# A graph network's two attention convolutions: selection matrices built by ScalarE instead of VectorE, and batch weights read from a PSUM bank

## The chip, the cores and the metric

The kernel runs on one core of a Trainium2 chip. A core has five engines, each with its own instruction queue that is worked off in order: TensorE (PE; its weight loads are listed as PEld), VectorE (DVE), ScalarE (ACT), GpSimd (POOL) and SyncE (SP). SP and POOL mainly issue transfers between the chip's main memory and the on-chip memory SBUF. TensorE writes its results into a second on-chip memory, PSUM, which is made of banks of 512 fp32 columns on 128 partitions; VectorE and ScalarE read and write both memories. Engines tell each other by semaphores that a piece of work is done. The metric is the time on the device in microseconds (us), the median of several runs; one further run was profiled.

## The reference

A graph has 12500 nodes with 128 features each and 200000 edges, sorted by their destination. The reference does a normalisation, two transformer convolutions (4 heads of 32), a second normalisation and a tensor product that is summed over the edges. One convolution is, for all edges at once:

```
q = (x @ Wq + bq); k = (x @ Wk + bk); v = (x @ Wv + bv)      # by node, heads x 32
e = ea @ We                                                   # ea: one number an edge
alpha = sum(q[dst] * (k[src] + e)) / sqrt(32)                 # by edge and head
p = exp(alpha - segment_max(alpha, dst)[dst])
w = p / segment_sum(p, dst)[dst]
out = segment_sum((v[src] + e) * w, dst) + x @ Ws + bs
```

The last stage gathers node rows by `src`, multiplies them with nine edge numbers and sums the products by `dst`.

## The kernel before, in words

Edges are worked on in groups of 4 tiles (U) of 128 edges, 391 groups in all. Three stages follow each other: convolution 0, convolution 1 (`conv(li)`), and the tensor product. Each runs once over all groups. In a convolution a step `s` of the loop works on several groups at once, each in another phase; the order of the instructions on every engine is the order in which the program writes them (a manual schedule, no planner).

What happens to group g in a convolution:

- `fetch_kv` (step g-3): GpSimd gathers the rows of k and v by `src`, with four indirect transfers, one a tile (`gather`, line 602, tile `kv`). For odd g the first of them waits for the last matmul of `query(g-3)`; the source calls that a pause for TensorE's results.
- `turn` (step g-2): ScalarE builds the selection matrix `OT` (destination rows by edges): |row - partition| into `off` (line 850), then relu(1 - off) (line 852).
- `query` (step g-1): TensorE multiplies `OT` with a window of q rows (line 823), which gives q for each edge, in two PSUM banks out of a ring of four (`bank`, tile `pq`).
- `scores` (step g): VectorE multiplies q with k (lines 883, 885) and adds up by head (line 887).
- Batches of 8 groups then get the maximum and the weights in nine steps: transposes by TensorE (`tops_turn`, `ends_turn`, `ends_back`, `weights_back`), scans and comparisons by VectorE (`tops_scan`, `ends_chain`, `weigh`), copies and exponentials by ScalarE (lines 917, 948, 949, 973). `weights_back` (line 978) transposes the weights into PSUM and `weights_keep` (line 984) lets ScalarE copy them into the SBUF tile `wt`.
- `messages` (15 or more steps after the group's scores): VectorE multiplies v with the weights (line 839) and writes the weights themselves and their products with the edge number (line 840).
- `hot`, one step ahead of the messages that need it: VectorE compares the numbers 0 to 127 with each edge's destination row in the group's window (`one_hot`, line 595). This is the selection matrix `O`, edges by destination rows, in a ring of three tiles.
- `sum_up` (lines 860, 862): TensorE multiplies `O` with the messages, which sums them by destination, with one more product that carries a sum over the group's border. `keep_sums` (line 867): ScalarE copies the result out of PSUM one step later, and SP stores it.

Beside the edges the loop works on windows of 128 nodes, about one in four steps: in convolution 0 `nodes_asked` (q of convolution 0) and `nodes_between` (mean, transposition, the skip product `x @ Ws`, q, k and v of convolution 1), in convolution 1 `nodes_mixed` (mean, normalisation with a square root by ScalarE, line 727, and a product). The skip product goes to PSUM (line 693) and VectorE adds it to x (line 698).

PSUM in a convolution: `wb` is one bank. It holds the transposed weights `pp` (columns 0 to 127), the small transposes `sm` of `ends_turn` and `ends_back` (columns 128 to 255) and two places for skip products. `nd` is another bank, with three places for transposes of node windows. Four banks are the ring `pq`, two the sums `pa`.

In the tensor product stage ScalarE builds `O`: for each tile |row - 0..127| into `off` (line 1136) and relu(1 - off) over the group (line 1138). There `products` forms four products a tile, by ScalarE (line 1147) and VectorE (lines 1151 to 1162, with one operand in PSUM), and TensorE sums them (line 1171).

Of the kernel before, what the change touches and what calls it, by code (L numbers as in the profile page):

```python
# [491 lines left out]
SLACK = 3  # L492
KVS = 5
REACH = 10
HEAD = 48
KW = 7
MIX = 352
# [36 lines left out]
def sorted_path(ctx: ExitStack, tc: tile.TileContext, sh_: Shared, x, edge_attr, out):  # L534
# [18 lines left out]
    GE = U * P  # L553
# [22 lines left out]

    SPE = mybir.EngineType.SP
    window = lambda t, w: t[w * P:(w + 1) * P, :]
    iob = sh_.iota
    rel_d, RG = sh_.rel_d, 2  # L580

    for i in range(2):
# [8 lines left out]

    def one_hot(pool, g, hot_bufs):

        O = pool.tile([P, U, P], F32, name="O", bufs=hot_bufs)
        nc.vector.tensor_tensor(O, iob[:, None, :].to_broadcast([P, U, P]),  # L595
                                REL[:, g * U:(g + 1) * U, None].to_broadcast([P, U, P]), op=OP.is_equal)
        return O

    def gather(t, rows, g, behind=None):
# [67 lines left out]
    def nodes_between(pool, bank, turned, skipped, w):  # L667

        A = pool.tile([P, SW], F32, name="A", bufs=4)
        s1 = pool.tile([P, D], F32, name="s1", bufs=4)  # L670
        xt = pool.tile([P, D], F32, name="xt", bufs=7)
        st = {}

        def load():
            nc.sync.dma_start(A, window(sum_d[0], w))
            nc.sync.dma_start(s1, window(s1_d, w))
            load_x(xt, w)

        def mean():
            h = node_mean(pool, 0, A)  # L680
            nc.vector.tensor_add(h, h, s1)
            nc.vector.tensor_add(xt, xt, sh_.BS)
            st["h"] = h

        def turn():
            nc.tensor.transpose(turned, st["h"], ident)

        def keep():
            st["hT"] = pool.tile([P, P], F32, name="hT", bufs=3)
            nc.scalar.copy(st["hT"], turned)  # L690

        def project():
            nc.tensor.matmul(skipped, st["hT"], sh_.WS, start=True, stop=True)
            st["at"] = bank()
            nc.tensor.matmul(st["at"][:, 0:AW], st["hT"], sh_.WA, start=True, stop=True)

        def evict():
            nc.vector.tensor_add(xt, xt, skipped)
            st["qkv"] = pool.tile([P, AW], F32, name="qkv", bufs=3)
            nc.vector.tensor_add(st["qkv"], st["at"][:, 0:AW], sh_.BA)  # L700

        def store():
            nc.sync.dma_start(window(kv_d[1], w), st["qkv"][:, QD:AW])
            nc.sync.dma_start(window(q_d[1], w), st["qkv"][:, 0:QD])
            nc.sync.dma_start(window(xs_d, w), xt)

        return [(0, "load", load), (1, "late", mean), (2, "early", turn), (3, "late", keep), (4, "early", project),
                (5, "late", evict), (6, "load", store)]

# [67 lines left out]
    def conv(li):  # L777
# [1 line left out]

        pool = ctx_l.enter_context(tc.tile_pool(name=f"fc{li}", bufs=1))  # L780
        ps = ctx_l.enter_context(tc.tile_pool(name=f"fcp{li}", bufs=1, space=bass.MemoryType.PSUM))
        wb = ps.tile([P, 512], F32, name="wb")
        pp, sm = wb[:, 0:U * BG * H].rearrange("p (u g h) -> p u g h", u=U, h=H), wb[:, 128:256]
        nd = ps.tile([P, 512], F32, name="nd")
        bank = lambda: ps.tile([P, 512], F32, name="pq", bufs=4)
        pps, outs, msgs, pas, asked = {}, {}, {}, {}, {}
        before = pool.tile([1, H], F32, name="before", bufs=2)
# [54 lines left out]
            return msg  # L842

        def hot(g):
            Os[g] = one_hot(pool, g, 3)

        def turn(g):

            off = pool.tile([P, GE], F32, name="off", bufs=1)
            nc.scalar.activation(off, rows[g // RG][:, g % RG * GE:(g % RG + 1) * GE], AF.Abs, bias=sh_.less)  # L850
            OTs[g] = pool.tile([P, U, P], F32, name="OT", bufs=3)
            nc.scalar.activation(OTs[g].rearrange("p u e -> p (u e)"), off, AF.Relu, bias=sh_.one, scale=-1.0)  # L852
# [121 lines left out]

        def weights_back(j):
            n = sizes[j]
            for u in range(U):
                nc.tensor.transpose(pp[:, u, 0:n, :].rearrange("p g h -> p (g h)"),
                                    bst[j]["aT"][0:n * H, u * P:(u + 1) * P], ident[0:n * H, 0:n * H])

        def weights_keep(j):
            n = sizes[j]
            pps[j] = pool.tile([P, U, BG, H], F32, name="wt", bufs=2)
            nc.scalar.copy(pps[j][:, :, 0:n, :], pp[:, :, 0:n, :])  # L984

        ends_at = {starts[j] + sizes[j] - 1: j for j in range(NB)}
        nodes = (nodes_between, nodes_mixed)[li]
# [24 lines left out]
        with tc.manual_schedule():  # L1012
            for s in range(-AHEAD, last):
                ended = [ends_at.get(s - k) for k in range(9)]
                rs = sums.get(s - 2, [])
                stored += len(rs)
                for k, (g, w) in enumerate(windows):
                    if g > stored or s >= NGR and k:
                        del windows[0:k]
                        break  # L1020
                    n = count % 2 * P
                    count += 1
                    for d, place, f in nodes(pool, bank, nd[:, n:n + P], wb[:, 256 + n:256 + n + P], w):
                        plan.setdefault((s + d, place), []).append(f)
                else:
                    windows = []
                run(s, "store")
                q = s + AHEAD
                if 0 <= q < NGR and rs:
                    bq, br = bases(2 * q, 2 * q + 1)  # L1030
                    assert q - rs[0] == LAG + AHEAD + 2
                    store_sums(rs[0], br)
                else:
                    for r in rs:
                        br, = bases(2 * (r + LAG + AHEAD + 2) + 1)
# [12 lines left out]
                if 0 <= s + 3 < NGR:  # L1048
                    fetch_kv(s + 3)

                if ended[2] is not None:
                    tops_keep(ended[2])
                if ended[6] is not None:
                    ends_keep(ended[6])
                if ended[8] is not None:
                    weights_keep(ended[8])
                if 0 <= s + 2 < NGR:
                    turn(s + 2)
                for m in sums.get(s - 1, []):
                    keep_sums(m)  # L1060

                if ended[1] is not None:
                    tops_turn(ended[1])
                if ended[3] is not None:
                    ends_turn(ended[3])
                if ended[5] is not None:
                    ends_back(ended[5])
                if ended[7] is not None:
                    weights_back(ended[7])
                run(s, "early")  # L1070
                for m in sums.get(s, []):
                    sum_up(m, messages(m))
                while hots and hots[0][1] <= s + 1:
                    hot(hots.pop(0)[0])
                if 0 <= s < NGR:
                    scores(s)
                if ended[2] is not None:
                    tops_scan(ended[2])
                if ended[4] is not None:
                    ends_chain(ended[4])  # L1080
                if ended[6] is not None:
                    weigh(ended[6])
                run(s, "late")
                if 0 <= s + 1 < NGR:
                    query(s + 1)
            assert not windows and not hots
# [9 lines left out]
    with tc.tile_pool(name="tp", bufs=1) as pool, \  # L1096
# [34 lines left out]
            gather(hgs[g], hm_d, g, summed.get(g - REACH - 2) if g % 2 else None)  # L1131

        def hot(g):
            off = pool.tile([P, U, P], F32, name="off")
            for u in range(U):
                nc.scalar.activation(off[:, u, :], iob, AF.Abs, bias=REL[:, g * U + u:g * U + u + 1], scale=-1.0)  # L1136
            Os[g] = pool.tile([P, U, P], F32, name="O", bufs=6)
            nc.scalar.activation(Os[g].rearrange("p u e -> p (u e)"), off.rearrange("p u e -> p (u e)"), AF.Relu,  # L1138
                                 bias=sh_.one, scale=-1.0)

        def products(g):
            j = batch_of[g]
# [531 lines left out]
```

## Time and profile before

| | us |
|---|---|
| median of 3 runs (7340.25 to 7360.03) | 7359.88 |
| profiled execution, its own time | 7424.75 |
| its span | 7422.9 |
| gathers of convolution 0, first start to last end | 137.5 to 2506.0 |
| gathers of convolution 1 | 2594.4 to 4961.4 |
| gathers of the tensor product | 5057.1 to 7356.6 |

| engine | busy us | of it |
|---|---|---|
| TensorE | 5031.8 | sums at L1171 1608.3, at L862 1424.7, queries at L823 1125.1 |
| VectorE | 4923.4 | prod 648.2, AL 549.6, O 532.2, msg 531.8 |
| ScalarE | 3053.5 | OT 564.5, off (L850) 560.5, M 495.7, off (L1136) 495.3 |
| GpSimd | 4867.4 | gathers 3291.2 and 1490.6 |

How to read it: a line of the profile's groups names the program's line, the engine and operation, what is written from what with sizes, and how often; then the busy time of all, the mean duration of one, and the idle time of the engine just before them, with what ended most of it. The span is the stretch between the first and the last instruction. "remote" names a release for which the profile has no sender. Where instructions overlap in an engine's pipeline, their busy time divided by their count is less than the mean of one.

### The profile page before, as it was taken

To read this page: it belongs to the slowest core of one execution; us is meant where nothing else is said; L and a number is where in the kernel's file an instruction comes from. 1 tells how busy PE (TensorE), PEld (TensorE's weight loads), DVE (VectorE), ACT (ScalarE), POOL (GpSimd) and SP (SyncE) were. 2 spreads that over 40 slices of the span, in tenths; PEclk is the share of its full clock that TensorE was granted. 3 is DMA by queue.
4 is the path that set the end of the run, shared out by engine and by line. 5 is a ranking of instruction groups with operands and counts; after the bars stand their busy time and mean duration, and the time that the engine had idled before them with its cause. 6 is when DMAs were issued, how large, how long until landed. Compare 5 with 4: busy or idle time off the path is not lost.

```text
span 7422.9 us, 89199 instructions
## 1 busy us (share of the span) xinstructions
PE 5031.8 (68%) x21249; PEld 3219.3 (43%) x21250; DVE 4923.4 (66%) x13362; ACT 3053.5 (41%) x7785; POOL 4867.4 (66%) x4779
## 2 busy tenths in 40 slices
PE   5566666666777646665666666665777787777777
PEld 4454555555555444444454545452233333333332
DVE  5566666777777746666676777774566666666666
ACT  3333333333333223333444444443555555555554
POOL 6676667676666367767666776654566666666664
PEclk8677777787777867777777777777888888888888
DMA  6455555566666445555555555544455555555554
GB/s 186 135 149 150 148 158 160 162 167 164 168 177 174 129 134 138 143 143 143 146 152 152 153 156 160 157 135 121 125 137 142 144 145 147 149 149 151 152 153 116
DMA packets 868134, 1107.31 MB, mean 149 GB/s; under 512 B 143858, under 2 KB 631568, under 8 KB 867603
## 3 DMA queue, kind: packets, MB, share of 16 engines
q0 software_dynamic: 250240, 692.16, 34.6%
q1 hardware_dynamic: 615832, 408.51, 19.8%
q8 instruction: 176, 2.88, 0.2%
q14 instruction: 355, 2.91, 0.1%
q10 hardware_dynamic: 1531, 0.84, 0.0%
HBM read 935.35 MB, written 165.60 MB: 148 GB/s over the span
## 4 chain that ended last, share of the span: by engine, by line
PE 27%; DVE 22%; another core or an unknown queue 17%; issue 15%; POOL 7%; ACT 6%; DMA 3%; SPq 1%; DVEq 0%; POOLq 0%; ACTq 0%
PE pa L862 8%; PE pa L1171 7%; PE pq L823 6%; POOL kv L602 5%; DVE prod L883 3%; DVE msg L839 2%; ACT M L1147 2%; ACT off L1136 2%; PE pa L860 2%; DVE O L595 2%; POOL hg L602 2%; DVE AL L887 2%; DMA kv<-fkv,srcI 1%; DVE tops L970 1%
## 5 line engine op out<-in xcount | busy, mean ns | idle before, releaser
L602 POOL DMA_INDIRECT kv<-fkv,srcI x3128 | 3291.2, 1052 | 1540.4 <-issue 893.0
L602 POOL DMA_INDIRECT hg<-fhm,srcI x1564 | 1490.6, 953 | 904.6 <-issue 506.0
L1171 PE MATMUL pa<-M,O 128*128 128x512 f32 x3128 | 1608.3, 661 | 295.8 <-ACT M L1147 87.5
L862 PE MATMUL pa<-msg,O 128*128 128x136 f32 x6256 | 1424.7, 363 | 374.1 <-issue 135.2
L883 DVE TENSOR_TENSOR prod<-pq,kv 128x256 f32<-128x256 f32 x1564 | 648.2, 416 | 1333.6 <-remote 737.4
L862 PEld LDWEIGHTS pa<-msg,O 128*128 128x128 f32 x6256 | 1108.1, 244 | 770.0 <-issue 549.3
L823 PE MATMUL pq<-qw,OT 128*128 128x132 f32 x6256 | 1125.1, 332 | 430.0 <-remote 124.3
L823 PEld LDWEIGHTS pq<-qw,OT 128*128 128x128 f32 x6256 | 1034.8, 244 | 471.1 <-remote 207.1
L1171 PEld LDWEIGHTS pa<-M,O 128*128 128x128 f32 x3128 | 624.4, 210 | 1042.5 <-issue 659.0
L852 ACT ACTIVATE OT<-off,fone 128x512 f32<-128x512 f32 x782 | 564.5, 722 | 334.0 <-remote 210.3
L1175 DVE TENSOR_REDUCE acc<-pa 128x128 f32<-128x512 f32 x391 | 265.4, 679 | 603.3 <-remote 448.9
L867 ACT COPY acc<-pa 128x136 f32<-128x136 f32 x782 | 203.6, 261 | 998.1 <-remote 489.4
L850 ACT ACTIVATE off<-rows,fless 128x512 f32<-128x512 bf16 x782 | 560.5, 717 | 106.1 <-DMA rows<-rel_d 67.5
L1147 ACT ACTIVATE M<-hg,s 128x128 f32<-128x128 f32 x1564 | 495.7, 388 | 193.3 <-remote 141.9
L887 DVE TENSOR_REDUCE AL<-prod 128x16 f32<-128x528 f32 x782 | 549.6, 703 | 27.1
L839 DVE TENSOR_TENSOR msg<-kv,wt 128x512 f32<-128x512 f32 x782 | 531.8, 680 | 34.0 <-ACT wt L984 17.3
L595 DVE TENSOR_TENSOR O<-fiota,REL 128x512 f32<-128x512 f32 x782 | 532.2, 681 | 9.4 <-PE pa L862 9.4
L1136 ACT ACTIVATE off<-fiota,REL 128x128 f32<-128x128 f32 x1564 | 495.3, 387 | 0.6 <-ACT M L1147 0.2
L1138 ACT ACTIVATE O<-off,fone 128x512 f32<-128x512 f32 x391 | 282.2, 722 | 273.2 <-remote 226.7
L1158 DVE TENSOR_TENSOR M<-hg,sh 128x384 f32<-128x384 f32 x782 | 392.5, 539 | 0.0
L860 PE MATMUL pa<-msg,fCAR 128*1 128x136 f32 x1196 | 286.7, 329 | 0.0
L1123 ACT COPY d<-sh 128x32 f32<-128x32 f32 (+3 forms) x50 | 9.2, 185 | 647.7 <-remote 448.4
(238 smaller groups left out, 5102.7 us busy)
## 6 DMA issues: line engine op xcount, KB each, us to landing
rows<-rel_d SPq DMA_DIRECT2D x390, 256.0 KB
fsum<-acc SPq DMA_DIRECT2D x782, 68.0 KB
qw<-fq SPq DMA_DIRECT2D x782, 66.0 KB
kv<-fkv,srcI POOLq DMA_INDIRECT x3128
hg<-fhm,srcI POOLq DMA_INDIRECT x1564
fout<-acc SPq DMA_DIRECT2D x391, 64.0 KB
fhm<-qkv SPq DMA_DIRECT2D x98, 176.0 KB
A<-fsum SPq DMA_DIRECT2D x196, 68.0 KB
```

The lines of the kernel that those rows point to most:

```text
L595: nc.vector.tensor_tensor(O, iob[:, None, :].to_broadcast([P, U, P]), REL[:, g * U:(g + 1) * U, None].to_broadcast([P, U, P]), op=OP.is_equal)
L602: i = nc.gpsimd.indirect_dma_start(out=t[:, u, :], out_offset=None, in_=rows[:, :], in_offset=bass.IndirectOffsetOnAxis(ap=srcI[:, g * U + ...
L823: asked[g] = nc.tensor.matmul(pqs[g][u // 2][:, u % 2, 0:QD], OT[:, u, :], qw, start=True, stop=True)
L839: nc.vector.tensor_mul(msg[:, :, :, 0:C], kv4(kv, D), wt[:, :, i, :, None].to_broadcast([P, U, H, C]))
L850: nc.scalar.activation(off, rows[g // RG][:, g % RG * GE:(g % RG + 1) * GE], AF.Abs, bias=sh_.less)
L852: nc.scalar.activation(OTs[g].rearrange("p u e -> p (u e)"), off, AF.Relu, bias=sh_.one, scale=-1.0)
L862: nc.tensor.matmul(pas[g], O[:, u, :], msg[:, u].rearrange("p h c -> p (h c)"), start=(u == 0), stop=(u == U - 1))
L883: nc.vector.tensor_mul(prod[:, c, :, 0:C], half[:, :, 0:D].rearrange("p u (h c) -> p u h c", h=H), kv4(kvs[g], 0)[:, c])
L887: nc.vector.tensor_reduce(ALs[j][:, :, i, :], prod, AX.X, OP.add)
L1136: nc.scalar.activation(off[:, u, :], iob, AF.Abs, bias=REL[:, g * U + u:g * U + u + 1], scale=-1.0)
L1147: nc.scalar.activation(M[:, u, 0, :], hg[:, u, 0:P], AF.Copy, scale=s0[:, i * U + u:i * U + u + 1])
L1171: summed[g] = nc.tensor.matmul(pas[g], O[:, u, :], M[:, u], start=(u == 0), stop=(u == U - 1))
```

## The change

- `one_hot`, called in all three stages now, builds `O` on ScalarE as the tensor product stage did: four |.| instructions into `off` and one relu(1 - off). VectorE's comparison is gone. `off` is one tile that `turn` and `one_hot` share in a convolution. The ring of `O` stays three tiles there (`HOTS`) and six in the last stage.
- `weights_keep` and the tile `wt` are gone. `weights_back` writes the weights of batch j into place j % 2 of `wb`, and `messages` reads them there.
- `wb` now holds two places for weights and one for skip products. While the gathers of the edges run (s below NGR) skip products go there, after that into the ring `pq`. `sm` moves to the fourth place of `nd`.
- Within a step, `messages` is written ahead of TensorE's transposes and of the node work placed "early"; `sum_up` stays behind these.

```diff
 def one_hot(pool, g, hot_bufs):
+    off = pool.tile([P, U, P], F32, name="off")
+    for u in range(U):
+        nc.scalar.activation(off[:, u, :], sh_.iota, AF.Abs, bias=REL[:, g * U + u:g * U + u + 1], scale=-1.0)
     O = pool.tile([P, U, P], F32, name="O", bufs=hot_bufs)
-    nc.vector.tensor_tensor(O, iob[:, None, :].to_broadcast([P, U, P]),
-                            REL[:, g * U:(g + 1) * U, None].to_broadcast([P, U, P]), op=OP.is_equal)
+    nc.scalar.activation(O.rearrange("p u e -> p (u e)"), off.rearrange("p u e -> p (u e)"), AF.Relu,
+                         bias=sh_.one, scale=-1.0)
     return O
...
 # nodes_between
-    nc.tensor.matmul(skipped, st["hT"], sh_.WS, start=True, stop=True)
+    st["skip"] = skipped()[:, 0:D]
+    nc.tensor.matmul(st["skip"], st["hT"], sh_.WS, start=True, stop=True)
...
 # conv
-    wb = ps.tile([P, 512], F32, name="wb")
-    pp, sm = wb[:, 0:U * BG * H].rearrange("p (u g h) -> p u g h", u=U, h=H), wb[:, 128:256]
+    wb = ps.tile([P, 4, P], F32, name="wb")
     nd = ps.tile([P, 512], F32, name="nd")
+    sm = nd[:, 3 * P:4 * P]
...
-    off = pool.tile([P, GE], F32, name="off", bufs=1)
+    off = pool.tile([P, U, P], F32, name="off").rearrange("p u e -> p (u e)")
...
 def weights_back(j):
     n = sizes[j]
+    pps[j] = wb[:, j % 2, :].rearrange("p (u g h) -> p u g h", u=U, h=H)
     for u in range(U):
-        nc.tensor.transpose(pp[:, u, 0:n, :].rearrange("p g h -> p (g h)"),
+        nc.tensor.transpose(pps[j][:, u, 0:n, :].rearrange("p g h -> p (g h)"),
                             bst[j]["aT"][0:n * H, u * P:(u + 1) * P], ident[0:n * H, 0:n * H])
-
-def weights_keep(j):
-    n = sizes[j]
-    pps[j] = pool.tile([P, U, BG, H], F32, name="wt", bufs=2)
-    nc.scalar.copy(pps[j][:, :, 0:n, :], pp[:, :, 0:n, :])
...
-    for d, place, f in nodes(pool, bank, nd[:, n:n + P], wb[:, 256 + n:256 + n + P], w):
+    for d, place, f in nodes(pool, bank, nd[:, n:n + P], bank if s >= NGR else lambda: wb[:, 2, :], w):
...
-    if ended[8] is not None:
-        weights_keep(ended[8])
...
     for m in sums.get(s - 1, []):
         keep_sums(m)
+    msgs_ = [(m, messages(m)) for m in sums.get(s, [])]
...
     run(s, "early")
-    for m in sums.get(s, []):
-        sum_up(m, messages(m))
+    for m, msg in msgs_:
+        sum_up(m, msg)
     while hots and hots[0][1] <= s + 1:
         hot(hots.pop(0)[0])
```

More of the change, by code (lines that the diff above doesn't have):

```diff
@@ L494 @@
 REACH = 10
+HOTS = 3
 HEAD = 48
@@ L578, in sorted_path @@
     window = lambda t, w: t[w * P:(w + 1) * P, :]
-    iob = sh_.iota
     rel_d, RG = sh_.rel_d, 2
@@ L697, in evict @@
         def evict():
-            nc.vector.tensor_add(xt, xt, skipped)
+            nc.vector.tensor_add(xt, xt, st["skip"])
             st["qkv"] = pool.tile([P, AW], F32, name="qkv", bufs=3)
@@ L844, in hot @@
         def hot(g):
-            Os[g] = one_hot(pool, g, 3)
+            Os[g] = one_hot(pool, g, HOTS)
         def turn(g):
-            off = pool.tile([P, GE], F32, name="off", bufs=1)
+            off = pool.tile([P, U, P], F32, name="off").rearrange("p u e -> p (u e)")
             nc.scalar.activation(off, rows[g // RG][:, g % RG * GE:(g % RG + 1) * GE], AF.Abs, bias=sh_.less)
@@ L1133, in hot @@
         def hot(g):
[L1134 to L1139, printed above, removed]
+            Os[g] = one_hot(pool, g, 6)
         def products(g):
```

## The prediction

> **What bounds the kernel now.** I read the page's busy times first, then the costliest groups, the busy time by stage, the chain that ended last and the waits, and last a stretch in order of time.
>
> ```profile
> PE 5031.8 (68%) x21249; PEld 3219.3 (43%) x21250; DVE 4923.4 (66%) x13362; ACT 3053.5 (41%) x7785; POOL 4867.4 (66%) x4779
> ...
> PE 27%; DVE 22%; another core or an unknown queue 17%; issue 15%; POOL 7%; ACT 6%; DMA 3%; SPq 1%; DVEq 0%; POOLq 0%; ACTq 0%
> PE pa L862 8%; PE pa L1171 7%; PE pq L823 6%; POOL kv L602 5%; DVE prod L883 3%; DVE msg L839 2%; ACT M L1147 2%; ACT off L1136 2%; PE pa L860 2%; DVE O L595 2%; POOL hg L602 2%; DVE AL L887 2%; DMA kv<-fkv,srcI 1%; DVE tops L970 1%
> ...
> L602 POOL DMA_INDIRECT kv<-fkv,srcI x3128 | 3291.2, 1052 | 1540.4 <-issue 893.0
> L602 POOL DMA_INDIRECT hg<-fhm,srcI x1564 | 1490.6, 953 | 904.6 <-issue 506.0
> ...
> L883 DVE TENSOR_TENSOR prod<-pq,kv 128x256 f32<-128x256 f32 x1564 | 648.2, 416 | 1333.6 <-remote 737.4
> ...
> L852 ACT ACTIVATE OT<-off,fone 128x512 f32<-128x512 f32 x782 | 564.5, 722 | 334.0 <-remote 210.3
> ...
> L839 DVE TENSOR_TENSOR msg<-kv,wt 128x512 f32<-128x512 f32 x782 | 531.8, 680 | 34.0 <-ACT wt L984 17.3
> L595 DVE TENSOR_TENSOR O<-fiota,REL 128x512 f32<-128x512 f32 x782 | 532.2, 681 | 9.4 <-PE pa L862 9.4
> L1136 ACT ACTIVATE off<-fiota,REL 128x128 f32<-128x128 f32 x1564 | 495.3, 387 | 0.6 <-ACT M L1147 0.2
> L1138 ACT ACTIVATE O<-off,fone 128x512 f32<-128x512 f32 x391 | 282.2, 722 | 273.2 <-remote 226.7
> ...
> L1158 DVE TENSOR_TENSOR M<-hg,sh 128x384 f32<-128x384 f32 x782 | 392.5, 539 | 0.0
> ```
>
> No engine is full, and the chain passes through all of them; O, the line that leaves VectorE, holds 2% of it (148 us). What matters is that a gather costs 1052 ns in the convolutions and 953 in the last stage. By stage:
>
> ```profile
> 300.00:2400.00 2100.00, 1424.33 (x7453) 1091.45 (x7454) 1467.14 (x4145) 696.58 (x1671) 1460.62 (x1385) 0.78 0.59 161
> 2800.00:4800.00 2000.00, 1271.52 (x6725) 992.00 (x6723) 1361.40 (x3950) 816.37 (x1751) 1390.16 (x1318) 0.75 0.54 149
> ```
>
> The columns are PE, PEld, DVE, ACT and POOL busy, then clock, DMA share and GB/s. Convolution 0 and 1 load VectorE and ScalarE differently, yet take 1.517 and 1.518 us a gather. So I took the gathers' start times, eight by eight (two groups, from one pause at line 602 to the next). The mean block is 12.14 and 12.15 us: 8 x (0.953 + 0.305 between) = 10.06, some 0.82 by which gathers are longer than 953 ns, and 1.26 of pause. The pause waits for `query(g-3)`, but in 87% and 83% of blocks its last matmul had ended before the block was issued, by 3.3 us at the median. What is late is TensorE's signal:
>
> ```profile
> 350.87 0.95 POOL L602 DMA_INDIRECT kv<-fkv,srcI  x1 [0.30 <-issue]
> 355.02 0.27 ACT L867 COPY acc<-pa 128x136 f32<-128x136 f32 x1 [12.85 <-remote]
> 355.08 0.42 DVE L883 TENSOR_TENSOR prod<-pq,kv 128x256 f32<-128x256 f32 x1 [15.94 <-remote]
> ```
>
> TensorE's matmuls ended at 343.5; ScalarE and VectorE stood until 355, after the block's gathers. These are the "remote" waits. Behind such a signal stand VectorE's `scores` and ScalarE's `keep_sums`, and the two steps of a block run in bursts after it. In convolution 0 half the blocks end within 11.88 to 12.25 us of their start, whether their gathers were issued in 9.9 us or in 11.
>
> **The change, part by part.** The profiled execution took 7424.75 us (span 7422.9): 137.5 until the first gather, 2368.5 for convolution 0's gathers, 88.4 until the next ones, 2367.0, 95.7, 2299.5 for the last stage's, and the end. The runs' median is 7359.88, 0.9913 of it; the sum is made on the former and scaled.
>
> *O leaves VectorE*: 782 x 0.681 = 532 us of it, 1.36 us a block, ahead of `scores`. *ScalarE takes it*: as in lines 1136 and 1138, whose busy times make 495.3/1564 = 0.317 (387 ns each, overlapped) and 0.722, so 4 x 0.317 + 0.722 = 1.99 us a group, 1556 us in all, less 25 for the copies of `wt`. ScalarE goes from 4.0 to 8.0 us of a 12.1 us block in convolution 0 and from 5.0 to 8.9 in convolution 1. Its cover is ScalarE's idle time in front of `keep_sums` (998 us at L867). Behind `hot` on ScalarE stand the `pen` and `c3` copies, the exponentials, node work and the next `turn`; TensorE's transposes and `sum_up` wait for those. After a late signal, a plain block before ran scores 1.85, msg 0.86, O 0.68, scores 1.85, msg 0.86 = 6.1 us until the second `sum_up` could start. Now VectorE is there after 5.4, and ScalarE (acc 0.26, O 1.99, turn 1.44, acc 0.26, O 1.99) after 5.9: 0.2 us better; 0.7 to 1.4 better where VectorE's batch or node work makes it late. Sums and query add 2.9 (1.7 and 1.2 in the order of time), so 8.8 of the some 11.6 us until TensorE's next signals: 2.8 us of slack.
>
> *What that moves.* Early blocks average 11.87 us, all 12.14: late ones cost 0.27 x 391 = 105 us. With 24 and 30 late blocks among 178 looked at in each convolution, some 59 in all, and 0.9 us off each (O's 0.68 for one step, 1.36 for two, less where a block is late by less): -53 us.
>
> *The gathers.* 527 convolution gathers that met no VectorE work took 953 ns; those that met O or msg, but no scan, 169 ns more. Without O and with msg reading PSUM the mean excess should fall from 101 to 33 ns (the 1756 that met neither; scans L909, L912, L970 stay): 68 x 3128 = 213 us of GpSimd. The Trainium skill (SBUF — State Buffer, "Who interferes with whom") says a two-input VectorE instruction holds up a GpSimd one that reads SBUF, but also that `tensor_tensor` doesn't stall descriptor generation. By its second statement the gain is 0, by the row up to 213. I take the row for busy time. On the path I take little: shorter issue has not brought the signal earlier. Only the 23% of blocks without a pause pass 8 x 0.068 = 0.54 us on, and longer ones follow: half of 0.23 x 391 x 0.54 = -25 us.
>
> *Messages from PSUM.* L883 and L1158, one PSUM operand each, give 416 ns at 256 elements and 539 at 384; the line goes through 662 at 512, against 680 now: 782 x 0.018 = 14 us of VectorE's own time, nothing on the path. The small product stays near 183.
>
> *The shared bank.* The Trainium skill (PSUM — Partial Sum Buffer, "PSUM bank collisions raise a hardware error") asks for guarding by bank and quadrant, not by address; that speaks against weights and skips in one bank. The row is
>
> ```profile
> PE wb L922 <- DVE xt L698: 38.0, 10, 6.7
> ```
>
> a transpose into one part of `wb` waiting for a read of another (us in all, times, longest). By address the cost is 0. By bank, `messages(s+1)` waits for the skip matmul of step s. In convolution 0 I put its end, and the next TensorE signal after it, beside the next msg: 26% of 77 would be late, 0.81 us in the mean over all, 63 us (80 on 98 windows); behind it on VectorE stand `scores`, and TensorE's sums and the pause wait. About 0.3 of that falls into the slack's end: +25 us (0 to 80). In the other direction the skip and `weights_back` now wait for `messages(s)`, 0.6 and 0.7 to 1.1 us later than before, 145 us of TensorE delay in all, mostly in its idle time: +10. The first messages of a batch needed that signal before too, through the `wt` copy. `sm` in bank `nd` takes away the 38 us above, and now orders there against 287 transposes and their copies (L646, L686, L737): no row shows it; between those 38 us gained and as much lost I take 0. That `messages` now stands ahead of the transposes in the program moves nothing on VectorE, where only `hot` came between it and `scores`.
>
> *The two ends of the convolutions* (88 and 96 us) are VectorE's, some 9 of each 10 us. 16 and 17 O leave each, 11 us, against ScalarE's 2.25 us a sum where two run a step: -5 each, -10. No DMA is added or moved; SP's queue is as before, GpSimd's only through its pause.
>
> Sum: -53 - 25 + 25 + 10 - 10 = -53; 7424.75 - 53 = 7371.75, times 0.9913: **7307 us**.
>
> **The rivals.** *Gathers set the pace after all*: then 213 us come off beside the 53: 7424.75 - 266 = 7159, scaled 7096; with half of the 213, 7265, scaled 7202. I place it at 7150. For it: GpSimd runs 90% of a block's time up to the pause. Against: the fixed 12 us.
>
> *ScalarE gets late (slower).* Line 727's square root waits for VectorE's node statistics (177 us at L727), loads a table (1283 ns) and now stands before the next O, likewise the exponentials. 2.8 us of slack decide. VectorE reaches a window's square root 3.9 us after the signal (scores 1.85, the node rows 2.0), load and root (1.28, 0.30) make 5.4, turn, acc and O 9.1, sums and query 12.0: 0.4 over the 11.6. At half the TensorE clock (0.75 is the mean) sums and query take 4, and it is 1.5 over. I take 0.5, since chain and exponential steps carry no load. 98 windows in convolution 1 and some 96 such steps in each convolution, 290 x 0.5 = +145, in place of the 53 gained, the rest cancelling: 7570, scaled 7504. If only those in a block's first step cost, 7497, scaled 7432. I place it at **7465**.
>
> *It changes nothing*: the signal's 12 us stay and late blocks stay late for another reason: 7360.
>
> **How the numbers follow.** My case 0.40, gathers 0.20, ScalarE late 0.26, nothing 0.14. A change under 0.3% (22 us, 7338 to 7382) can't be told from none. Faster: 0.38 of mine, the gathers' 0.20, 0.02 of "nothing": 0.60. Slower: 0.25 of ScalarE's. Same: 0.02, 0.01 and 0.12: 0.15. The likeliest case alone spans 7260 to 7340. For 8 in 10: 7150, above which half the cases with shorter gathers lie, to 7455, below which some 0.16 of ScalarE's 0.26 lie.
>
> **What would show it.** kv gathers near 985 ns (right), 1052 (the contention is something else); ScalarE busy near 4585 us; msg at 660; O's four forms at 387 and 722. Blocks still near 11.9 us mean my bound holds; near 11.3, the first rival. ScalarE ahead of TensorE's O in the waits (little now) is the second. A wait of msg on TensorE's skip shows the bank. My weakest step is that the signal's delay doesn't follow the gathers' issue: blocks with long gathers are also those in which VectorE was let run.

## The result, and the profile after

The changed kernel takes 7398.68 us (median of twelve executions, 7388.73 to 7431.86), the kernel before 7361.70 beside it (twelve, 7340.25 to 7389.97): a ratio of 1.0051, with an interval of 1.0038 to 1.0065. It is slower by 37 us, or 0.5%. The prediction was 7307 us and faster.

The numbers that follow have two levels: in some sittings (one chip, both kernels executed in turn) the kernel before takes 7360 to 7440 us, in others 6575 to 6598, and the executions of a sitting agree within 1%; what tells the levels apart is shown below. The comparison above, and the profile that the prediction read, are of the upper level. At the lower level the same two kernels give 6333.23 against 6581.79, a ratio of 0.9623 (0.9610 to 0.9636).

The page of the changed kernel at the upper level; line numbers moved by 3 to 5 (L602 is L605, L883 is L887, L978 is L983):

```profile
PE 5053.3 (68%) x21249; PEld 3244.2 (44%) x21250; DVE 4449.6 (60%) x12580; ACT 4512.2 (61%) x11595; POOL 4635.2 (63%) x4779
...
PE 34%; DVE 21%; another core or an unknown queue 16%; issue 14%; ACT 6%; POOL 4%; DMA 3%; SPq 1%; DVEq 0%; POOLq 0%; ACTq 0%
...
L605 POOL DMA_INDIRECT kv<-fkv,srcI x3128 | 3057.8, 978 | 1783.6 <-issue 860.2
L605 POOL DMA_INDIRECT hg<-fhm,srcI x1564 | 1491.0, 953 | 861.6 <-issue 495.7
...
L887 DVE TENSOR_TENSOR prod<-pq,kv 128x256 f32<-128x256 f32 x1564 | 647.9, 417 | 1862.2 <-remote 809.8
...
L843 DVE TENSOR_TENSOR msg<-kv,wb 128x512 f32<-128x512 f32 x782 | 525.9, 672 | 14.5 <-PE pa L864 8.8
...
L983 PE MATMUL wb<-fident,aT 32*128 32x32 f32 (+3 forms) x400 | 54.1, 265 | 357.7 <-DVE msg L844 186.5
```

VectorE lost 474 us of work, and GpSimd's gathers in the convolutions fell from 1052 to 978 ns, as the prediction had it; but the idle time before `prod` grew by 529 us (1333.6 to 1862.2), and GpSimd's before the gathers by 243 (1540.4 to 1783.6), more than the gathers' busy time fell (233). What was saved has become waiting. The busy time by stage says the same (PE, PEld, DVE, ACT and POOL busy, clock, DMA share, GB/s): in 2100 us of convolution 0 GpSimd issues 1370 gathers and other work, where it was 1385, and in convolution 1 1323 where it was 1318.

```profile
300.00:2400.00 2100.00, 1387.65 (x7372) 1075.45 (x7373) 1244.85 (x3762) 1326.78 (x3327) 1339.60 (x1370) 0.78 0.57 159
2800.00:4800.00 2000.00, 1292.56 (x6738) 1010.14 (x6736) 1160.21 (x3621) 1427.70 (x3359) 1295.10 (x1323) 0.76 0.53 149
```

The gathers of convolution 0 span 2397 us (before 2368), of convolution 1 2352 (2367), of the last stage, whose code did not change, 2260 (2300). The profiled executions themselves, 7390.34 and 7424.75, stand the other way round than the medians: that of before lies 63 us above its median and above all of its twelve executions, and its last stage is 40 us longer than the changed kernel's. So the 37 us of the medians can't be read off one pair of traces. What both traces give for the convolutions alone is +13 us, and it is taken apart below. Had the other 23 of the 63 us fallen into the convolutions too, it would be +36; that is an estimate, and no trace shows where they fell.

### The profile page after: what moved, and what is told of

The parts are those of the page before. It is cut to its first block, busy times and chain, and to the rows that moved or that the text cites. A ratio compares the mean times of both kernels' runs of the same rounds, so it can differ in the third digit from the quotient of the medians.

```text
span 7388.4 us, 92525 instructions
## 1 busy us (share of the span) xinstructions
PE 5053.3 (68%) x21249; PEld 3244.2 (44%) x21250; DVE 4449.6 (60%) x12580; ACT 4512.2 (61%) x11595; POOL 4635.2 (63%) x4779
## 4 chain that ended last, share of the span: by engine, by line
PE 34%; DVE 21%; another core or an unknown queue 16%; issue 14%; ACT 6%; POOL 4%; DMA 3%; SPq 1%; DVEq 0%; POOLq 0%; ACTq 0%
PE pa L1165 12%; PE pa L866 9%; PE pq L827 6%; POOL kv L605 3%; DVE prod L887 3%; DVE msg L843 2%; ACT off L596 2%; PE pa L864 2%; DVE AL L891 2%; DVE tops L974 2%; DMA kv<-fkv,srcI 1%; DVE M L1152 1%; ACT M L1141 1%; DVE top L913 1%
## 5 line engine op out<-in xcount | busy, mean ns | idle before, releaser
L605 POOL DMA_INDIRECT kv<-fkv,srcI x3128 | 3057.8, 978 | 1783.6 <-issue 860.2
L605 POOL DMA_INDIRECT hg<-fhm,srcI x1564 | 1491.0, 953 | 861.6 <-issue 495.7
L1165 PE MATMUL pa<-M,O 128*128 128x512 f32 x3128 | 1629.4, 669 | 321.1 <-DVE acc L1169 135.8
L887 DVE TENSOR_TENSOR prod<-pq,kv 128x256 f32<-128x256 f32 x1564 | 647.9, 417 | 1862.2 <-remote 809.8
L596 ACT ACTIVATE off<-fiota,REL 128x128 f32<-128x128 f32 x4692 | 1492.4, 390 | 1.0 <-ACT M L1141 0.4
L598 ACT ACTIVATE O<-off,fone 128x512 f32<-128x512 f32 x1173 | 846.6, 722 | 199.3 <-remote 133.0
L843 DVE TENSOR_TENSOR msg<-kv,wb 128x512 f32<-128x512 f32 x782 | 525.9, 672 | 14.5 <-PE pa L864 8.8
L983 PE MATMUL wb<-fident,aT 32*128 32x32 f32 (+3 forms) x400 | 54.1, 265 | 357.7 <-DVE msg L844 186.5
```

Source lines behind the costliest of these rows:

```text
L596: nc.scalar.activation(off[:, u, :], sh_.iota, AF.Abs, bias=REL[:, g * U + u:g * U + u + 1], scale=-1.0)
L598: nc.scalar.activation(O.rearrange("p u e -> p (u e)"), off.rearrange("p u e -> p (u e)"), AF.Relu, bias=sh_.one, scale=-1.0)
L605: i = nc.gpsimd.indirect_dma_start(out=t[:, u, :], out_offset=None, in_=rows[:, :], in_offset=bass.IndirectOffsetOnAxis(ap=srcI[:, g * U + ...
L843: nc.vector.tensor_mul(msg[:, :, :, 0:C], kv4(kv, D), wt[:, :, i, :, None].to_broadcast([P, U, H, C]))
L887: nc.vector.tensor_mul(prod[:, c, :, 0:C], half[:, :, 0:D].rearrange("p u (h c) -> p u h c", h=H), kv4(kvs[g], 0)[:, c])
L1165: summed[g] = nc.tensor.matmul(pas[g], O[:, u, :], M[:, u], start=(u == 0), stop=(u == U - 1))
```

## The experiments

Theories at the start: the **shared bank** (TensorE's weights and skips wait for `messages`, and fall late), **ScalarE** (its queue is late with `O`), and the **signal** (shorter gathers buy nothing, because TensorE's signals reach the other engines only when a block of eight gathers is through).

### The parts one at a time, and the kernel before again

The comparison alone (the kernel before with the new `one_hot`):

```diff
-    nc.vector.tensor_tensor(O, iob[:, None, :]..., REL[...]..., op=OP.is_equal)
+    for u in range(U):
+        nc.scalar.activation(off[:, u, :], sh_.iota, AF.Abs, bias=REL[...], scale=-1.0)
+    nc.scalar.activation(O..., off..., AF.Relu, bias=sh_.one, scale=-1.0)
```

> Only the comparison moves to ScalarE; weights are copied to SBUF and skips stay where they were in the kernel before. Shared bank theory (the loss comes from TensorE's weights and skips waiting for messages): the loss is gone, 7310 to 7350 us, 10 to 50 below before, and the waits of weights_back on msg are absent. ScalarE theory (its queue is late with the comparison): the whole loss is here, about 7395. Signal theory (shorter gathers buy nothing, TensorE's signal comes 12 us after a block's start in any case): 7345 to 7375, kv gathers near 985 ns, fewer than 10% of the blocks without a pause instead of 20 to 26%.

The weights alone (the changed kernel with VectorE's comparison put back):

> Only messages from PSUM, with the new places of weights, skips and small products; the comparison stays on VectorE. Shared bank theory: as slow as after or slower, 7390 to 7430, with 150 us or more of weights_back waiting for msg and 30 to 40% late blocks in convolution 0 instead of 13%. ScalarE theory: 7350 to 7365. Signal theory alone: 7360, with gathers between 985 and 1052 ns.

The comparison on VectorE, with one tensor operand:

```diff
-    nc.vector.tensor_tensor(O, iob[:, None, :]..., REL[...]..., op=OP.is_equal)
+    for u in range(U):
+        nc.vector.tensor_scalar(O[:, u, :], iob, REL[:, g * U + u:g * U + u + 1], None, op0=OP.is_equal)
```

> The kernel before with the comparison still on VectorE, as four instructions with one tensor operand each and the tile number as a scalar operand, so that O no longer reads two tensors of SBUF while gathers run. If the two-tensor reads lengthen the gathers, kv gathers fall from 1052 to about 1000 ns. Signal theory: the time stays within 20 us of before all the same (plus what the four instructions take over 681 ns, at most 782 x 0.3 us of VectorE's, of which a tenth shows). If shorter gathers are worth their time: 7280 or below.

And the kernel before, for a second profile:

> The kernel before once more, for a second profile. If the profiled 7424.75 us with its 2299.5 us in the last stage was one slow execution, this one has about 2260 there and about 7360 to 7390 in all; convolutions 2368 and 2367 within 10 us, and 13 and 17% late blocks within 3 points.

The sitting was of the lower level, while what was expected of these runs had been worked out for the upper one: before 6577.74, the comparison alone 6410.87 (0.9741, 0.9727 to 0.9754), the weights alone 6446.01 (0.9797, 0.9783 to 0.9810), the four instructions 6448.69 (0.9800, 0.9787 to 0.9813). The page of before there:

```profile
DMA 26%; POOL 25%; DVE 22%; issue 15%; PE 6%; ACT 3%; SPq 1%; DVEq 0%; POOLq 0%; ACTq 0%
...
L602 POOL DMA_INDIRECT kv<-fkv,srcI x3128 | 3327.7, 1064 | 1040.5 <-issue 864.5
...
L883 DVE TENSOR_TENSOR prod<-pq,kv 128x256 f32<-128x256 f32 x1564 | 651.3, 417 | 914.3 <-DMA kv<-fkv,srcI 755.1
```

The 17% of "another core or an unknown queue" are gone, and with them the "remote" waits. A gather costs the same (1064 ns against 1052), so does `prod`, and TensorE's sums at L862 take 358 ns a matmul against 363; what differs is when TensorE's signal arrives. I took, in both traces, the start of ScalarE's copy of a sum (L867) against the later of two ends, that of the last matmul of the sum and that of ScalarE's work ahead of it: at the upper level 22% of the 782 copies start more than 1 us after both and 13% more than 3 us, at the lower level none does. At the lower level no block of eight gathers has a pause; the query that the next pause asks for had ended 1.7 us before the block itself began, in the median. So the "fixed 12 us" of the prediction are a property of the sitting. I call the two **held** (upper) and **at once** (lower).

The granted TensorE clock differs as well. These are the rows of the two pages of before (40 slices of the span, in tenths of full speed), the held one first:

```profile
PEclk8677777787777867777777777777888888888888
PEclk8687878788888867777878878887999999999999
```

Over the span it is 0.79 to 0.80 in the held traces and 0.85 to 0.87 in the others. In the last stage, whose work is the same in all the kernels, it is 0.86 to 0.87 where signals are held and 0.98 to 0.99 at once, and that stage's gathers span 2250 to 2300 us against 1966 to 1971. A slow clock at that moment isn't what holds a signal: in the held trace of before, 24% of the copies came over 1 us late when the clock had been full for the 3 us before their sum ended (277 copies), and 15% when it had been half (227). Whether the lower clock makes signals late in some other way or follows from the waiting is not shown. And the profile models the ends of matmuls, so it can't rule out that a matmul itself ended later than it says.

The changed kernel was then timed in an at-once sitting:

> The changed kernel, unaltered, beside the kernel before. The last call's kernel before took 6577.74 us, with 'remote' gone from its waits and no pause at any block's start; the 7360 us of the first comparison has 17% remote in the chain. Where TensorE's signals come at once, gathers are the bound (rival: gathers set the pace): each part alone gave -167 and -132 us, together they should give 8 x (0.953 + 0.305) + 0.2 = 10.26 us a block, 391 x (10.98 - 10.3) = -266 us, 6310 us or a ratio of 0.96. Where the signals are held up, the ratio stays at 1.005 and the time at 7399.

It took 6333.23 against 6581.79. Its page:

```profile
POOL 24%; DMA 23%; DVE 18%; issue 16%; PE 9%; ACT 8%; SPq 1%; DVEq 0%; POOLq 0%; ACTq 0%
...
L605 POOL DMA_INDIRECT kv<-fkv,srcI x3128 | 3066.6, 980 | 1050.7 <-issue 872.2
...
L887 DVE TENSOR_TENSOR prod<-pq,kv 128x256 f32<-128x256 f32 x1564 | 653.2, 419 | 1060.2 <-DMA kv<-fkv,srcI 643.8
...
L983 PE MATMUL wb<-fident,aT 32*128 32x32 f32 (+3 forms) x400 | 51.8, 258 | 338.7 <-DVE msg L844 247.0
```

Here the rival "gathers set the pace" holds: gathers 84 ns shorter, times 3128, make 263 us, and 249 were measured. TensorE's weights wait 247 us for `messages`, more than in the held sitting, and beside what the gathers gain no cost of it shows.

### What shortens the gathers

Weights from PSUM, comparison on VectorE as four instructions (both edits above in one kernel):

> Weights and skips read from the PSUM bank as in the changed kernel, but the comparison stays on VectorE, as four instructions with one tensor operand each (304 ns apart measured, 900 ns a group against 681). Where TensorE's signals come at once (before at 6580 us): if the gain is only that nothing with two SBUF tensors runs beside the gathers, gathers fall to about 985 ns and the time to 6320 to 6360, as with the comparison on ScalarE (6333); if it is that VectorE was relieved, 6440 or more. Where signals are held up (before at 7360): shared bank theory 7395 to 7430, as slow as the changed kernel although ScalarE has no more to do than before; ScalarE theory 7345 to 7370.

At once: 6373.98 against 6575.29 (0.9695, 0.9682 to 0.9708), gathers 987 ns; 6320 to 6360 had been expected. And the changed kernel with the first scan of a batch reading PSUM:

```diff
-    nc.scalar.copy(b["aT"][0:R], b.pop("at")[0:R])
+    nc.scalar.copy(b["aT"][0:R], b["at"][0:R])
...
-    nc.vector.tensor_tensor_scan(top[0:R], seg[0][0:R, 0:GE], b["aT"][0:R], -BIG, ...)
+    nc.vector.tensor_tensor_scan(top[0:R], seg[0][0:R, 0:GE], b.pop("at")[0:R], -BIG, ...)
```

> The changed kernel with the first scan of a batch (line 913) reading its scores in the PSUM bank where TensorE turned them, instead of ScalarE's copy; the copy stays for the later steps. It takes one of the two-tensor instructions away that still lengthen gathers. Signals at once (after 6333): of the 0.2 us a block by which gathers still exceed 953 ns, the first scan holds 31 of some 83 us in all, so 6300 to 6330. Signals held up (after 7399): if fewer meetings of gathers and VectorE make it worse, 7395 to 7415; if shorter gathers help, below 7390.

At once: 6323.45 against 6576.66 (0.9611, 0.9598 to 0.9625), gathers 979 ns. The intervals of the two ratios overlap (0.9610 to 0.9636 for the change), so no gain is shown: against before of their sittings the medians differ by 5 us, where I had given 31 to that scan. All at-once sittings together, with gathers from one profile each:

| kernel | gather, ns | shorter by, x 3128 | against before of its sitting, us |
|---|---|---|---|
| before | 1064 | | |
| weights alone | 1016 | 150 | -132 (later -143, -143, -145) |
| comparison on VectorE, four instructions | 1016 | 150 | -129 |
| comparison alone, on ScalarE | 1012 | 163 | -167 (later -173) |
| weights, and four instructions | 987 | 241 | -201 |
| both (the change) | 980 | 263 | -249 |
| both, scan from PSUM | 979 | 266 | -253 |
| both, useless work on VectorE, one tensor (below) | 985 | 247 | -232 (later -222) |

The time follows the gathers' length, whether ScalarE or VectorE makes `O`, so most of what is gained at once is that gathers no longer meet two-tensor instructions of VectorE. It is not all: the 48 us between the two ways of making `O` with the weights (-201 and -249) are more than the 22 that their gathers differ by, and so are the 38 without the weights (-129 and -167, where the gathers give 13). VectorE's own time may be the rest; that is not shown.

### The shared bank, where signals are held

Two banks for the weights; the two places of the sums share one in return:

```diff
-wb = ps.tile([P, 4, P], F32, name="wb")
+wbs = [ps.tile([P, 4, P], F32, name=f"wb{i}") for i in range(2)]
+sums_at = ps.tile([P, 2, 256], F32, name="pa")
...
-pas[g] = ps.tile([P, SW], F32, name="pa", bufs=2)
+pas[g] = sums_at[:, g % 2, 0:SW]
...
-pps[j] = wb[:, j % 2, :]...
+pps[j] = wbs[j % 2][:, 0, :]...
```

> The changed kernel with the weights of even and odd batches in two banks and the skip in the one whose weights messages are not reading then; the bank that this takes comes from the sums, whose two places now lie in one bank. So weights_back and the skip no longer wait for messages of the same step; the sums may wait for ScalarE's copy of the last one instead. Where TensorE's signals come at once (before at 6580, after at 6333): the waits of weights_back on msg (247 us there) go, but TensorE runs ahead there: 6320 to 6335. Where they are held up (before at 7360, after at 7399): shared bank theory 7300 to 7355, with late blocks back from 40 to some 13% in convolution 0; ScalarE theory 7390 to 7410; signal theory alone 7350 to 7375.

Held: 7384.41 against 7359.64 (1.0035, 1.0021 to 1.0049). The wait is gone from `weights_back`, whose idle time now ends with ScalarE's exponential, but the sums wait for the copy of the last sum, and longer:

```profile
PE pa L868 <- ACT acc L873: 550.5, 230, 14.7
...
PE wb L985 <- ACT aT L979: 134.2, 46, 6.6
```

(us in all, times, longest.) One wait was traded for another, so this one decides little; it leaves most of the loss in place. The decision came from the parts alone in held sittings. The comparison:

> Only the comparison on ScalarE, asked again for the case of held-up signals, which the two runs of it so far did not meet (0.974 of before each). Held signals (before 7360): if O beside the gathers is what helped, 7375 to 7400, late blocks in convolution 0 above 25%; shared bank theory 7310 to 7355; no cause of loss in this part 7355 to 7365. Signals at once: 0.974 again.

7435.86 against 7438.71 (0.9998, 0.9984 to 1.0012). VectorE is relieved here as much as in the changed kernel (4462 us busy, there 4450):

```profile
PE 5083.0 (68%) x21249; PEld 3259.7 (44%) x21250; DVE 4462.0 (60%) x12580; ACT 4518.9 (61%) x11695; POOL 4720.6 (64%) x4779
...
L605 POOL DMA_INDIRECT kv<-fkv,srcI x3128 | 3143.5, 1005 | 1695.7 <-issue 875.4
```

The weights, which at once gave 6443.80, 6455.75 and 6438.40 us in three more sittings (0.9781, 0.9789, 0.9786):

> The weights alone, asked for held-up signals again. If the loss is this part's own (the shared bank): 1.004 to 1.008 of before, weights_back waiting 100 us or more for msg, late blocks in convolution 0 above 30%. If it needs both parts: 0.998 to 1.002. Signals at once: 0.978 to 0.980.

7353.82 against 7362.73 (0.9988, 0.9977 to 0.9998).

```profile
PE wb L980 <- DVE msg L841: 122.1, 38, 7.2
```

The bank's wait is there, 122 us of it, and the kernel is not slower. Shorter gathers don't hide a cost of the bank: they take 1005 ns in both of these kernels, and the comparison alone gains nothing by it. **The weights with the shared bank cost nothing that can be measured alone, and ScalarE's comparison alone costs nothing either.** Together the two should give 0.9986; they give 1.0051. Both single-cause theories fall.

### What the two together take away

With both parts VectorE has 474 us less to do, and gathers meet neither `O` nor `msg`. First both are given back, by a comparison whose result nobody reads:

```diff
 Os[g] = one_hot(pool, g, HOTS)
+spare = pool.tile([P, U, 112], F32, name="spare")
+nc.vector.tensor_tensor(spare, sh_.iota[:, None, 0:112]..., REL[...]..., op=OP.is_equal)
```

> The changed kernel plus, on VectorE, a comparison whose result nobody reads (4 x 112 elements, two SBUF tensors, some 600 ns, 782 times): it gives VectorE its old load back and lengthens gathers as before, while ScalarE and the bank stay as in the changed kernel. Where TensorE's signals come at once (before 6580, after 6333): gathers back to about 1035 ns and 391 x 0.65 = some 200 us lost, 6480 to 6560, although VectorE is not the bound there. Where signals are held up (before 7360, after 7399): if long gathers let signals through in the middle of a block, blocks without a pause come back to some 20% and the time falls to 7350 to 7385; if the loss is VectorE's or the bank's, 7400 to 7460.

Held: 7364.93 against 7360.62 (1.0005, 0.9992 to 1.0019), gathers 1001 ns.

```profile
L605 POOL DMA_INDIRECT kv<-fkv,srcI x3128 | 3132.0, 1001 | 1677.6 <-issue 874.6
...
L851 DVE TENSOR_TENSOR spare<-fiota,REL 128x448 f32<-128x448 f32 x782 | 479.4, 613 | 0.4
```

More work on VectorE, longer gathers, and the changed kernel is faster by 0.5%. But the blocks without a pause did not come back as that theory asked (1% and 11% of the blocks of the two convolutions; 20% and 26% before the change). So VectorE's load was given back alone:

```diff
 Os[g] = one_hot(pool, g, HOTS)
+spare = pool.tile([P, U, 112], F32, name="spare")
+for u in range(2):
+    nc.vector.tensor_scalar(spare[:, 2 * u:2 * u + 2, :], sh_.iota[:, None, 0:112]...,
+                            REL[:, g * U + u:g * U + u + 1], None, op0=OP.is_equal)
```

> The changed kernel plus, on VectorE, a comparison whose result nobody reads, as long as the one of the run before (some 600 ns a group, in two instructions) but with one tensor operand, so that it doesn't lengthen gathers. Held signals (before 7360, after 7399; with the two-tensor comparison 7365): if the longer gathers were what helped, 7390 to 7410 and kv gathers stay at 980 ns; if it was VectorE's delay, 7355 to 7375. Signals at once (before 6580, after 6333): gathers stay at 980 ns and the time at 6333 to 6380; VectorE has room.

At once: 6354.89 against 6586.39 (0.9655, 0.9641 to 0.9669), gathers 985 ns, and 0.9656 in a second sitting. There VectorE's 474 us cost about 20. Held:

> The one-tensor comparison on top of the changed kernel, asked once more for held-up signals (twice it met signals at once: 0.9655 and 0.9656). Held signals: 1.003 to 1.006 if gathers of 980 ns are what loses, 0.998 to 1.002 if it is VectorE's missing load. Signals at once: 0.9655 again.

7369.75 against 7364.90 (1.0003, 0.9990 to 1.0016), with gathers as short as in the changed kernel:

```profile
L605 POOL DMA_INDIRECT kv<-fkv,srcI x3128 | 3057.7, 978 | 1763.1 <-issue 873.1
...
L852 DVE TENSOR_SCALAR spare<-fiota,REL 128x224 f32<-128x224 f32 x1564 | 474.2, 343 | 0.4
```

So it is not the gathers' length that loses. **Where signals are held, what costs 0.5% is a VectorE that has less to do, or comes sooner to `scores`, together with the weights' edits.** Neither does it alone: with the comparison alone VectorE is relieved as much and nothing is lost, and with the weights alone it has its old load and nothing is lost. Which of the weights' edits it takes (the shared bank, the new places of skips and small products, `messages` written earlier) is not shown; two banks for the weights took away little.

### What it does to the blocks

A block is the eight gathers from one pause to the next; it is late if the query that the next pause waits for ends after the eighth gather. The table has 356 blocks of the two convolutions from each held trace:

| kernel | without a pause, conv 0 and 1 | late, of 356 | on time, us | late, us | ratio |
|---|---|---|---|---|---|
| before | 20%, 26% | 53 | 11.95 | 13.30 | 1 |
| both (the change) | 3%, 8% | 120 | 11.82 | 12.92 | 1.0051 |
| both, two banks | 2%, 5% | 107 | 11.82 | 13.02 | 1.0035 |
| both, spare with two tensors | 1%, 11% | 77 | 11.81 | 13.12 | 1.0005 |
| both, spare with one tensor | 1%, 1% | 78 | 11.84 | 13.06 | 1.0003 |
| comparison alone | 3%, 8% | 76 | 11.96 | 12.98 | 0.9998 |
| weights alone | 7%, 16% | 67 | 11.77 | 13.07 | 0.9988 |

Among the six changed kernels the ratio falls as the number of late blocks does, but for one step of 77 to 78. A block on time hardly moves, with gathers between 978 and 1052 ns. The row of before is from the long execution of 7424.75 us, and that of the comparison alone from a sitting in which before took 7439; both have a last stage of 2288 to 2300 us, the other five one of 2250 to 2262. So rows are best compared within the five. There the changed kernel and the two with useless work differ in their late blocks and not in those on time: 120 x 1.10, 77 x 1.31 and 78 x 1.22 us of lateness make 31 and 37 us less with the useless work, 34 and 40 over all 391 blocks, and by the ratios the time differs by 34 and 35.

The late blocks come in trains: in the changed kernel's convolution 0, 11 of the first 80 of these blocks and 53 of the last 74, where the windows of `nodes_between` are denser (27 of the 84 additions of a skip at L702 that run beside the gathers fall into the last sixth, 1 into the first). One of them, in order of time (start, duration, engine, line, and the idle time before with what ended it):

```profile
1874.69 0.95 POOL L605 DMA_INDIRECT kv<-fkv,srcI  x1 [3.57 <-PE pq L827]
...
1880.82 1.66 PE L827 MATMUL pq<-qw,OT 128*128 128x132 f32 x8
...
1884.31 0.50 PE L866 MATMUL pa<-msg,O 128*128 128x136 f32 x2
...
1886.02 0.42 DVE L887 TENSOR_TENSOR prod<-pq,kv 128x256 f32<-128x256 f32 x1 [6.47 <-PE pa L866]
...
1886.62 1.14 PE L827 MATMUL pq<-qw,OT 128*128 128x132 f32 x8 [1.82 <-PE pa L866]
...
1888.03 1.11 POOL L605 DMA_INDIRECT kv<-fkv,srcI  x1 [3.59 <-PE pq L827]
```

The query that VectorE needs had ended by 1882.48, the sums by 1884.81, and the eighth gather is through at 1884.44; VectorE starts at 1886.02, after 6.47 us of idling. TensorE's next query starts only after the first part of `prod` (the ring `pq` has four banks, two a group), ends at 1887.76, and the next block begins at 1888.03, 13.34 us after this one. A late query makes the next signals late, which keeps VectorE late: that is how a train can hold, read from this stretch and not shown for all. Why a VectorE with less work falls into such trains more often is not settled, and the numbers are of one execution each: the one-tensor spare has 67 late blocks in convolution 0 and 11 in convolution 1. Not tried was a held kernel with VectorE's instructions moved and their load unchanged, which would separate its load from the time at which it reaches `scores`.

Nor is it settled what makes a sitting held or at once. The chip doesn't: four of the chips (2, 6, 10 and 11) gave both.

## Why the prediction was wrong

- **"Late blocks", -53 us, is the step that failed, in its sign.** It took blocks to be late because VectorE was behind, so that 0.9 us less work would bring each forward. In the held traces late blocks went from 53 to 120. With lateness 1.35 us a block before (13.30 - 11.95) and 1.10 after, that is 120 x 1.10 - 53 x 1.35 = +60 us over 356 blocks, +66 over all 391. The comparison alone, which takes `O` from VectorE and leaves the rest, gains nothing (0.9998, with 76 late blocks). And the two useless comparisons show the opposite of what was assumed: adding 474 to 479 us to VectorE takes the change's loss away. Why late blocks become more is open. (The 105 us that the prediction gave to late blocks count from blocks that are early by over 2 us, 11.87; against all that are on time the late ones cost 53 x 1.35 = 72, or 79 over 391.)
- **"The gathers", -25.** Gathers at 978 ns: foreseen (985). But the blocks without a pause, through which the gain was to pass, all but vanished (23% to 6%), and blocks on time became 0.13 us shorter instead, 391 x 0.13 = -51 us. Right in sign, half as large as measured. The two together, +66 - 51 = +15, are the +13 that the convolutions' gathers span more. Both rest on the long execution of before, so they divide those +13 us and not the 37 of the medians.
- **The shared bank, +25 and +10.** The wait of `messages` on the skip did not appear (L843 idles 14.5 us in all, 34 before). The one of `weights_back` on `messages`, put at +10 with the skip's, is 186.5 us of TensorE's waiting; alone (122 us) it costs nothing. The rule of the Trainium skill on guarding by bank (PSUM — Partial Sum Buffer, "PSUM bank collisions raise a hardware error") named a wait that is there, in the direction priced at +10 and not in the one priced at +25.
- **The contention itself** was read rightly: the row (169 ns) against the Trainium skill's remark that `tensor_tensor` doesn't stall descriptor generation (SBUF — State Buffer, "Who interferes with whom"). In both kinds of sitting gathers shorten by 74 to 84 ns when `O` and `msg` no longer read two SBUF tensors.
- **ScalarE**: 4512 us busy against 4585 foreseen, and not late: with the comparison alone it is as busy (4519) and there is no loss. That rival, given 0.26, named the right outcome for a wrong cause.
- **Tails**, -10: 84.9 and 92.8 us against 88.4 and 95.7, so -6.4. **msg**: 672 ns against 662.
- **"Gathers set the pace"** (0.20) has the right mechanism wherever signals come at once. That its full form, 7096 of 7360, is 0.964 and 0.9623 was measured is partly luck: its 266 us were 213 of gathers and 53 of late blocks, and at once before has no late block, while the gathers alone gave 263 (84 ns each, not 68). The prediction rejected it for the fixed 12 us, which it took for the chip's and which the one trace it had could not show to be otherwise.

The weakest step was named: that the signal's delay doesn't follow the gathers' issue. Where signals are held it stood (on-time blocks 11.77 to 11.96 us in all seven held traces); what failed is the belief that late blocks would follow VectorE's load.

## What to carry to other kernels

When a trace shows an engine released by nobody ("remote") long after its input was written, find out whether that delay is there in every sitting before taking it for the bound: the same change was worth -3.8% and +0.5%. Of the versions measured in both kinds of sitting, either part alone is level or faster (the weights 0.978 to 0.980 and 0.9988, the comparison 0.974 and 0.9998); the whole change is best at once (0.962) and worst held (1.0051). And relieving an engine that stands in a loop of waits can lose: test it by giving the load back as useless work, once with and once without the side effect (here, two tensor operands or one).

## What was not expected of the hardware

- TensorE's signals to ScalarE come either within 1 us of both engines being ready (782 of 782) or, in 22% of cases, later, with 13% over 3 us; the same kernel then takes 7360 instead of 6580 us, with a granted clock of 0.79 instead of 0.85. The level holds for a sitting and changes between sittings on the same chip.
- A tensor_scalar with one SBUF tensor on VectorE lengthens indirect gathers little: in the kernel with the one-tensor spare, held, the 179 that met it alone took 985 ns and the 537 that met no VectorE work 954, and the mean over all is 978 as without it. With a tensor_tensor of two tensors it is 1111 (146 gathers) against 953 (556), and 1001 over all; with `O` and `msg` 1052.
- 474 us of useless VectorE work made a kernel of 7399 us faster by 0.5%.
